# Turning the slots' token rows on VectorE, and packing expert weights from GpSimd, in a two-layer graph-attention and mixture-of-experts kernel

## The chip, the cores and the metric

The program runs on one core of one Trainium2 chip. The metric is the device time of one execution in microseconds (us), smaller is better. The engines of the core are named here as in the profile: PE is TensorE (matmuls; PEld is its weight load, which overlaps the matmuls), DVE is VectorE, ACT is ScalarE, POOL is GpSimd and SP is SyncE, which in this kernel does nothing but issue DMAs and read the registers they need. POOL and ACT can issue DMAs too.

## The reference

There are 2708 tokens of 256 numbers. Two layers follow one another; each has an attention over a graph (a 2708 by 2708 matrix of 0 and 1) and then a mixture of 8 experts of which every token uses two.

```python
# layer 0
x = x + elu(softmax(where(adj > 0, q @ k.T / 16, -9e15)) @ v)    # q, k, v from _layernorm(x)
# then, on t = _layernorm(x):
xn = layernorm(t)
xe[e] = xn * ln_g[e] + ln_b[e]
h = gelu(xe[e] @ W1[e] + b1[e])            # 256 -> 1024
y = h @ W2[e] + b2[e]                      # 1024 -> 256
x = x + sum over the top two experts of weight * y
# layer 1
x = x + softmax(where(adj > 0, s_src + s_dst, -1e9)) @ (t @ W_fc + b_fc)
x = x + sum over the top two experts of p_e * (gelu(t @ W1[e] + b1[e]) @ W2[e] + b2[e])   # 256 -> 512 -> 256
```

## The kernel before, in words

The work has five stages, one behind the other: attention of layer 0, expert slots of layer 0, attention of layer 1, expert slots of layer 1, and the final sum.

**Attention of layer 0** (`layer0_attention`). The queries are cut into six blocks of 512 (the last has 148); for each block `b` the loop runs over 22 key tiles `k`, and one pass of that loop is called a key step. A step computes the scores of one key tile on PE (L537), takes their exponential on ACT (L549), multiplies by the mask on DVE (L552), and adds the product with the values into accumulators on PE (L601), three steps later. Beside it, DVE makes the next block's masks out of integers loaded from `adj` (L386, L403, L409); the columns of the last two key tiles have their own small load, `load_apart` (L414), made in step 14 of a block and used by PE in steps 20 and 21 (L544, L576). One more job runs beside these steps, a list named `background` of which one entry is started every fifth step. Its entries are DMAs issued by SP: two fillers, and one `pack` for each of the 16 experts (8 in each layer), which copies that expert's `W1`, `W2`, `b2`, `b1` (and in layer 0 `ln_g`, `ln_b`) from their inputs into one DRAM row per partition, `packed`, by 4 or 6 DMAs (L1009 to L1025).

**Routing** (`route`, L1093). Each finished tile of 128 tokens is normalized (`norm_stats`, L245, which has one short POOL instruction, L256, and `normed`, L259), its two experts are chosen, and its rows are written by an indirect DMA from POOL (L1197) into `disp`, a DRAM tensor of 258 numbers per row: 256 of the token, then its index, then its weight. The rows of an expert are contiguous there. Routing is written as a generator whose pieces are placed between the steps of other work (`Line`).

**Slots** (`Experts.slots`, L1406). A slot is 128 rows of one expert. Layer 0 runs 45 of them, layer 1 runs 47, the last two of these inside a branch that is taken only when they are used. For a slot the kernel fetches weights (`fetch_weights`, L1356: an indirect DMA from POOL into one of 4 buffers, whose rows are skipped when the buffer already holds that expert) and rows (`fetch_rows`, L1373: one DMA of 128 rows of 1032 bytes from SP, into one of 6 buffers `xg`). Both are fetched three slots ahead (`AHEAD`). `turned` (L1410) turns the 128 by 256 rows into columns: two PE transposes against the identity into PSUM (L1414), then a copy out of PSUM, by DVE with the expert's own norm in layer 0 (L1418, two instructions) and by ACT in layer 1 (L1424). `up` multiplies by `W1` on PE (L1441) and takes the gelu on ACT (L1449); it also scales the bias, on DVE in layer 0 (L1432) and on ACT in layer 1 (L1434). `down` multiplies by `W2` on PE (L1457), and DVE scales and adds the bias (L1463); the result `y` goes out by an indirect DMA from POOL (L1469, L1476) at the row numbers that lie in `xg`. The PE work of `down` for one slot is put behind `up` of the next, so that ACT has time for the gelu.

The order of the instructions on each engine comes from a scheduler in layer 0, and from the order of the program on PE, ACT and DVE in the slots of layer 1 (L1399). SP's order is always that of the program.

Of the kernel before, what the change touches and what calls it, by code (L numbers as in the profile page):

```python
# [9 lines left out]
F32 = mybir.dt.float32  # L10
# [86 lines left out]
AHEAD = 3  # L97
DROW = D + 2
# [5 lines left out]
def adj_ffn_kernel(ctx: ExitStack, tc: tile.TileContext, a: dict, out: bass.AP):  # L104
# [156 lines left out]

    def to_columns(dst, src, r):

        tp = misc.tile([P, GROUP, P], F32, name="misc")
        for c in range(DC):
            nc.tensor.transpose(tp[:, c, :r], src[:, c * P : (c + 1) * P], ident[:r, :r])  # L266
        nc.scalar.copy(dst, tp[:, :DC, :r])
# [77 lines left out]
    def layer0_attention(line):  # L345
        with ExitStack() as scope, ExitStack() as until_last:
# [18 lines left out]
            xin = {}  # L365
# [164 lines left out]
            def scores(b, k, g, apart, mT):  # L530
                b0, nb, ts_ = BLOCKS[b]
                kr, k0 = ROWS[k], k * P
                if k == NT - 1:
                    return tail_scores(b, g, apart, mT)
                ps = ps_s.tile([P, BN], F32, name="s")
                for c in range(DC):
                    nc.tensor.matmul(  # L537
                        ps[:kr, :nb], xnT[:, c, k0 : k0 + kr], g[:, c, :nb],
                        start=(c == 0), stop=(c == DC - 1 and k < KEYS),
                    )  # L540
                if k >= KEYS:
                    for j, t in enumerate(ts_):
                        r = ROWS[t]
                        nc.tensor.matmul(  # L544
                            ps[:kr, j * P : j * P + r], apart[:, j, :kr], minus_big[:, :r],
                            start=False, stop=(j == len(ts_) - 1),
                        )
                p = of_block(b, "p", [P, nb], F32, bufs=6)
                nc.scalar.activation(p[:kr, :nb], ps[:kr, :nb], AF.Exp, scale=1.0 / 16.0)  # L549
                mask = MASKS[b].of_key(mT, k)  # L550
                if k < KEYS:
                    nc.vector.scalar_tensor_tensor(  # L552
                        p, p, LARGEST, mask, op0=ALU.min, op1=ALU.mult
                    )
                else:
                    nc.vector.tensor_scalar(
                        mask[:kr], ps[:kr, :nb], -BIG / 2, None, ALU.is_gt, saturate=False,
                    )
                return p

            def tail_scores(b, g, apart, mT):
# [23 lines left out]
                for n0, n1, r in parts_:  # L585
                    nc.scalar.activation(p[n0:n1, :r], ps[n0:n1, :r], AF.Exp, scale=1.0 / 16.0)
# [36 lines left out]
            def evict(b, accs, total):  # L623
                for j, t in enumerate(BLOCKS[b][2]):
                    raw = rows.tile([P, VALUES + 1], F32, name="raw", bufs=6)
                    (nc.scalar.copy if j % 2 else nc.vector.tensor_copy)(
                        raw[: ROWS[t], : D + 1], accs[j][: ROWS[t]]
                    )
                    line.add(finish(t, raw, total))
# [6 lines left out]
            for b, (b0, nb, ts_) in enumerate(BLOCKS):  # L636
# [4 lines left out]
                for k in range(NT):  # L641
# [10 lines left out]
                    if k == (0 if b == last else NT - 8):  # L652
# [21 lines left out]
                    if background and b > 0 and k % 5 == 1 and (b > 1 or k > 10):  # L674
                        background.pop(0)()
                    if b > 0:
# [322 lines left out]
    def pack_weights(name, hidden, own_norm):  # L999
# [9 lines left out]
        def pack(e):  # L1009
            to = packed[e * P : (e + 1) * P, :]  # L1010
            nc.sync.dma_start(
                to[:, :w2].rearrange("p (c h) -> p c h", c=DC),
                a[f"{name}_W1"][e].rearrange("(c p) h -> p c h", p=P),
            )
            nc.sync.dma_start(
                to[:, w2:b2].rearrange("p (f d) -> p f d", f=hc),
                a[f"{name}_W2"][e].rearrange("(f p) d -> p f d", p=P),
            )
            nc.sync.dma_start(to[:, b2:b1], a[f"{name}_b2"][e].partition_broadcast(P))
            nc.sync.dma_start(to[:, b1:ln], a[f"{name}_b1"][:, e, :])  # L1020
            if own_norm:
                with nc.allow_non_contiguous_dma(reason="a few small vectors"):
                    nc.sync.dma_start(to[:, ln : ln + DC], a[f"{name}_ln_g"][:, :, e])
                    nc.sync.dma_start(to[:, ln + DC : row], a[f"{name}_ln_b"][:, :, e])
        background.extend(partial(pack, e) for e in range(E))  # L1025
        return packed, hc, w2, b2, b1, ln, row

    class Experts:
        def __init__(self, layer, hidden, packed_weights, w_gate, gate_bias, own_norm, xd, disp, early):
# [7 lines left out]
            self.groups = [f"written{layer}", f"late{layer}", f"apart{layer}", f"after{layer}"]  # L1037
# [24 lines left out]
        def other_rows(self, start, late=True):  # L1062


            groups = [self.groups[0]] if late else []
            if self.begun:
                groups.append(self.groups[1])
            for group in groups:
                tc.declare_no_dep(start.ins, group=group, reason="other rows of disp")
                tc.add_to_no_dep_group(group, start.ins)  # L1070
# [22 lines left out]
        def route(self, t, x, logits=None):  # L1093
# [17 lines left out]
            if own_norm:  # L1111
                xt = rows.tile([P, D], F32, name="xn", bufs=4)[:r]
                normed(xt, x[:r], mean, once)
                normed(rows2[:r, 0, :D], x[:r], mean, twice)
            else:
                xt = rows2[:r, 0, :D]
                row = normed(xt, x[:r], mean, once)
# [201 lines left out]
        def begin_steps(self):  # L1319
# [3 lines left out]
            rows_ = [self.fetch_rows(s) for s in range(AHEAD)]  # L1323
            self.fetched = []
            for s in range(AHEAD):
                self.fetched.append((self.fetch_weights(s), rows_[s]))
# [46 lines left out]
        def fetch_rows(self, s):  # L1373
            disp = self.disp
            xg = self.one.tile([P, DROW], F32, name="xg", bufs=RING + 2)
# [5 lines left out]
            start = nc.sync.dma_start(xg, disp[bass.ds(at, P), :])  # L1381
            if s < FULL_AFTER[self.early]:
                self.other_rows(start, late=False)
            if s in (0, FULL_AFTER[self.early]):
                self.behind_written(start)
            return xg

        def run(self, line):
            with (
                self.scope,  # L1390
                tc.tile_pool(name="ffn2", bufs=2, side=self.side) as two,
                tc.tile_pool(name="ps_mm", bufs=2, space=PSUM) as ps_mm,
                tc.tile_pool(name="ps_tp", bufs=2, space=PSUM) as ps_tp,
                tc.tile_pool(name="ps_acc", bufs=2, space=PSUM) as ps_acc,
            ):
                with ExitStack() as order:
# [7 lines left out]
                    self.slots(two, ps_mm, ps_tp, ps_acc, line)  # L1404

        def slots(self, two, ps_mm, ps_tp, ps_acc, line):  # L1406
# [3 lines left out]
            def turned(s):  # L1410
                w, xg = self.fetched[s]
                tp = ps_tp.tile([P, GROUP, P], F32, name="tp")
                for c in range(DC):
                    nc.tensor.transpose(tp[:, c, :], xg[:, c * P : (c + 1) * P], ident)  # L1414
                xe = two.tile([P, DC, P], F32, name="xe")
                if own_norm:
                    for c in range(DC):
                        nc.vector.tensor_scalar(  # L1418
                            xe[:, c, :], tp[:, c, :],
# [3 lines left out]
                else:  # L1423
                    nc.scalar.copy(xe, tp[:, :DC, :])  # L1424
# [29 lines left out]
            def down(s, w, xg, hT, bias2, then):  # L1454
                ps = ps_acc.tile([P, D], F32, name="acc")
                for f in range(hc):
# [6 lines left out]
                nc.vector.scalar_tensor_tensor(  # L1463
                    y, ps, xg[:, D + 1 : D + 2], bias2, op0=ALU.mult, op1=ALU.add
                )
                at = bass.IndirectOffsetOnAxis(ap=xg.bitcast(I32)[:, D : D + 1], axis=0)
# [22 lines left out]
            def slot(s, s1):  # L1489
                nonlocal placed, behind, xe  # L1490
                w, xg = self.fetched[s]
# [4 lines left out]
                hT, bias2 = up(w, xe, xg[:, D + 1 : D + 2])  # L1496
# [4 lines left out]
                def fetch(behind_add=None):  # L1501
# [4 lines left out]
                    if s + AHEAD < SLOTS and s + AHEAD == len(self.fetched):  # L1506
                        self.fetched.append((
                            self.fetch_weights(s + AHEAD, behind_add), self.fetch_rows(s + AHEAD)
                        ))
# [16 lines left out]
                behind = (s, w, xg, hT, bias2)  # L1526
# [28 lines left out]
    background = []  # L1555
# [90 lines left out]
```

## Time and profile before

Six runs of the kernel have a median of 1245.55 us (1239.37 to 1250.77). The profiled execution took 1243.04 us, of which the profile shows a span of 1241.3 us.

| stage | from, us | to, us | PE busy, us |
|---|---|---|---|
| attention of layer 0 | 0 | 499 | 482.9 |
| slots of layer 0 | 499 | 837 | 335.0 |
| attention of layer 1 | 837 | 1014 | 171.5 |
| slots of layer 1 | 1014 | 1214.5 | 181.9 |
| final sum | 1214.5 | 1241.3 | 0 |

Over the span PE is busy for 1171.3 us, DVE for 539.7, ACT for 447.2 and POOL for 421.3. A line of a group of instructions reads: source line, engine, operation, output and inputs with their shapes, count, then busy time and the mean duration of one, then the idle time of the engine just ahead of them and what ended most of it. In a line of the timeline the first number is the start and the second the length of a run of like instructions, and a bracket gives the idle time ahead of it with what ended it. A busy PE is not PE at its peak, since matmuls are pipelined: what a matmul costs is the distance to the next start.

### The profile page before, as it was taken

The page shows a single profiled execution, that of the slowest core. Times are in us where ns is not written, and L with a number is a line of the kernel's source. Part 1 is how long each engine was busy: PE and PEld are TensorE (multiplying, and loading weights), DVE is VectorE, ACT ScalarE, POOL GpSimd, SP SyncE. Part 2 cuts the span into 40 slices and gives each one's busy share as a digit, 9 for nine tenths or more (in the row PEclk, how much of TensorE's full clock was granted, in tenths as well). Part 3 has the DMA queues.
Part 4 walks back from the last instruction along what each step waited for, and adds up shares of the span by engine and source line. Part 5 has one row for each costly group of instructions (what it writes and reads, how often), then busy time and mean ns, then how long its engine had stood idle before and what let it go on. Part 6 is the DMA issues. An engine that isn't in the chain of part 4 may idle for free. (4 is left out here: it accounts for less than half of the span.)

```text
span 1241.3 us, 20059 instructions
## 1 busy us (share of the span) xinstructions
PE 1171.3 (94%) x6712; PEld 941.2 (76%) x6712; DVE 539.7 (43%) x2055; ACT 447.2 (36%) x1301; POOL 421.3 (34%) x525
## 2 busy tenths in 40 slices
PE   8989999999999999999999999999999988899990
PEld 5656666666665675899999999987999977799880
DVE  5465762845456536631211121115867774211114
ACT  3222222222212222642233322324767657344440
POOL 3010020120211204343333333334635567455450
PEclk9999999999999999999999999998999999999995
DMA  9493973999997677475667745443004225644457
GB/s 201 67 182 83 166 171 113 200 215 228 217 192 168 131 174 261 138 210 141 226 203 230 271 124 176 111 107 92 2 10 156 102 65 192 173 142 139 136 183 276
DMA packets 148355, 197.83 MB, mean 159 GB/s; under 512 B 27595, under 2 KB 131748, under 8 KB 142104
## 3 DMA queue, kind: packets, MB, share of 16 engines
q1 hardware_dynamic: 120314, 110.16, 38.7%
q0 software_dynamic: 27040, 83.56, 21.8%
q10 hardware_dynamic: 894, 2.77, 0.6%
q8 instruction: 56, 0.92, 0.3%
q14 instruction: 51, 0.42, 0.1%
HBM read 263.66 MB, written 66.15 MB: 266 GB/s over the span
## 5 line engine op out<-in xcount | busy, mean ns | idle before, releaser
L1441 PE MATMUL mm<-xe,ring 128*128 128x128 f32 x2192 | 266.2, 278 | 15.4 <-ACT xe L1424 7.6
L1441 PEld LDWEIGHTS mm<-xe,ring 128*128 128x128 f32 x2192 | 255.2, 192 | 32.4 <-issue 19.2
L1457 PE MATMUL acc<-ring,hT 128*128 128x256 f32 x1096 | 261.3, 381 | 2.1 <-issue 1.6
L1449 ACT ACTIVATE hT<-mm,ring 128x128 f32<-128x128 f32 x548 | 156.0, 369 | 287.1 <-issue 179.7
L1463 DVE SCALAR_TENSOR_TENSOR y<-acc,xg,bias 128x256 f32<-128x256 f32 x92 | 44.5, 484 | 399.7 <-PE acc L1457 367.6
L1457 PEld LDWEIGHTS acc<-ring,hT 128*128 128x128 f32 x1096 | 198.4, 191 | 24.5 <-issue 1.9
L601 PEld LDWEIGHTS acc<-v,p 128*128 128x128 f32 (+1 forms) x880 | 159.5, 190 | 65.3 <-issue 41.0
L601 PE MATMUL acc<-v,p 128*128 128x257 f32 (+1 forms) x880 | 204.1, 384 | 2.4 <-DVE p L552 1.4
L537 PE MATMUL s<-g,xnT 128*128 128x512 f32 x420 | 202.6, 602 | 0.0
L1358 POOL DMA_INDIRECT ring<-L_ffn_packed,weight_row x98 | 103.5, 1056 | 185.2 <-issue 95.1
L256 POOL TENSOR_TENSOR ln_rs<-ln_rs,minus_half 128x2 f32<-128x2 f32 x88 | 66.0, 752 | 250.3 <-DVE ln_rs L252 212.2
L1197 POOL DMA_INDIRECT disp<-row,to x88 | 90.1, 1024 | 163.4 <-DVE to L1194 57.3
L844 PE MATMUL acc<-parts,m 128*128 128x266 f32 x924 | 127.6, 295 | 0.0
L549 ACT ACTIVATE p<-s 128x512 f32<-128x512 f32 x105 | 62.5, 595 | 180.5 <-PE s L537 145.4
L844 PEld LDWEIGHTS acc<-parts,m 128*128 128x128 f32 x924 | 118.2, 187 | 4.4 <-ACT raw L871 0.9
L537 PEld LDWEIGHTS s<-g,xnT 128*128 128x128 f32 x420 | 76.2, 192 | 53.7 <-issue 50.3
L552 DVE SCALAR_TENSOR_TENSOR p<-p,mT 128x512 f32<-128x512 f32 x100 | 68.4, 686 | 94.4 <-ACT p L549 91.0
L1476 POOL DMA_INDIRECT xd<-y,xg x45 | 71.4, 1586 | 87.1 <-issue 32.3
L811 ACT CAST m<-mT 128x512 fp32r<-128x512 fp8e4 (+4 forms) x168 | 71.9, 475 | 12.3 <-PE acc L844 7.2
L1469 POOL DMA_INDIRECT xd<-y,xg x47 | 47.0, 999 | 20.8 <-PE tp L1414 7.6
L403 DVE TENSOR_SCALAR m_rows<-adj 128x512 fp8e4<-128x512 int32 (+1 forms) x105 | 42.1, 433 | 2.0 <-DMA adj<-in_adj_dram 2.0
L1414 PE MATMUL tp<-ident,xg 128*128 128x128 f32 x184 | 35.1, 275 | 1.2 <-DMA xg<-disp 0.7
(252 smaller groups left out, 1080.1 us busy)
## 6 DMA issues: line engine op xcount, KB each, us to landing
adj<-in_adj_dram SPq DMA_DIRECT2D x100, 256.0 KB
L_ffn_packed<-in_L_ffn_W_dram SPq DMA_DIRECT2D x16, 1024.0 KB
xg<-disp SPq DMA_DIRECT2D x98, 129.0 KB
L_ffn_packed<-in_L_ffn_W_dram SPq DMA_DIRECT2D x16, 512.0 KB
neighbours<-mT SPq DMA_DIRECT2D x5, 1408.0 KB
mT<-neighbours SPq DMA_DIRECT2D x5, 1408.0 KB
xin<-in_x_dram SPq DMA_DIRECT2D x42, 128.0 KB
ring<-L_ffn_packed SPq DMA_DIRECT2D x4, 1154.0 KB
```

The costliest lines, as they stand in the source:

```text
L256: nc.gpsimd.tensor_tensor(rs[:r, 1], rs[:r, 0], minus_half[:r], ALU.pow)
L537: nc.tensor.matmul(ps[:kr, :nb], xnT[:, c, k0 : k0 + kr], g[:, c, :nb], start=(c == 0), stop=(c == DC - 1 and k < KEYS),)
L552: nc.vector.scalar_tensor_tensor(p, p, LARGEST, mask, op0=ALU.min, op1=ALU.mult)
L601: nc.tensor.matmul(accs[j][:r], p[keys, q0 : q0 + r], v[keys, k, :], start=(k == 0), stop=(k == NT - 1),)
L811: nc.scalar.copy(m[:, : q1 - q0], MASKS[b].of_key(mTs[b], k)[:, q0 - b * BN : q1 - b * BN],)
L844: nc.tensor.matmul(acc[:r], masks[t], parts[:, k, i], start=(k == 0 and i == 0), stop=False,)
L1197: nc.gpsimd.indirect_dma_start(disp[:], bass.IndirectOffsetOnAxis(ap=to[:r, j : j + 1], axis=0), rows2[:r, j], None,)
L1358: start = nc.gpsimd.indirect_dma_start(w, None, packed[:], bass.IndirectOffsetOnAxis(ap=self.weight_row[:, s : s + 1], axis=0), bounds_che ...
L1441: nc.tensor.matmul(ps[:, i, :], w[:, c * hidden + f * P : c * hidden + (f + 1) * P], xe[:, c, :], start=(c == 0), stop=(c == DC - 1),)
L1449: nc.scalar.activation(hT[:, f, :], ps[:, i, :], AF.Gelu, bias=w[:, b1 + f : b1 + f + 1])
L1457: nc.tensor.matmul(ps, hT[:, f, :], w[:, w2 + f * D : w2 + (f + 1) * D], start=(f == 0), stop=(f == hc - 1),)
L1476: start = nc.gpsimd.indirect_dma_start(xd[:], at, y, None, bounds_check=N - 1, oob_is_err=False, compute_op=ALU.add)
```

## The change

In the slots, PE no longer transposes the rows. DVE does it with its own transpose, which works on blocks of 32 by 32. For that, the token's numbers are written into `disp` in another order (`by_quarters`), and a slot's rows are loaded by four DMAs, each of which fills 32 partitions with pieces of 64 numbers (256 bytes), and a fifth that loads the last two numbers of each row into a buffer of its own, `who`. Rows are fetched five slots ahead, weights still three. In layer 0 the transpose of slots below 45 is put on DVE behind the result `y` of the slot two before (or, at the beginning, behind the copy of an accumulator of the attention). In layer 0 the norm now reads SBUF and not PSUM; in layer 1 the copy on ACT is gone. PSUM that held the transposes goes to `up`, which has 4 buffers and not 2.

The packing of the weights is cut into pieces (`W1`; `W2`; `b2` and `b1`; in layer 0 also `ln_g` and `ln_b`), 56 in all. From step 11 of block 1 on, each key step issues one piece, from POOL and not from SP, and each piece has to wait for the exponential of that step. `background` keeps the other entries. The small load `load_apart` is made in step 4 of a block and not in step 14.

```diff
+ROWS_AHEAD = 5
+    def in_chunks(x):
+        return x.rearrange("p (c g j) -> p g c j", c=DC, g=GROUP)
+    def by_quarters(row):
+        return row.rearrange("p (g c j) -> p g c j", g=GROUP, c=DC)
...
-                nc.scalar.activation(p[:kr, :nb], ps[:kr, :nb], AF.Exp, scale=1.0 / 16.0)
+                exp_of[0] = nc.scalar.activation(
+                    p[:kr, :nb], ps[:kr, :nb], AF.Exp, scale=1.0 / 16.0
+                )
...
+                    if j == 0:
+                        experts0.issued = copied
...
-                    if k == (0 if b == last else NT - 8):
+                    if k == (0 if b == last else GROUP):
                         apart = load_apart(b)
...
-                    if background and b > 0 and k % 5 == 1 and (b > 1 or k > 10):
+                    if background and b > 0 and k % 5 == 1:
                         background.pop(0)()
+                    if packing and b > 0 and (b > 1 or k > 10):
+                        for start in packing.pop(0)():
+                            tc.add_manual_dep(
+                                start.ins, exp_of[0].ins.name,
...
+                                reason="no sooner than this step",
+                            )
...
-            nc.sync.dma_start(
+        def pieces(e):
+            to, dma = packed[e * P : (e + 1) * P, :], nc.gpsimd.dma_start
+            yield lambda: [dma(
                 to[:, :w2].rearrange("p (c h) -> p c h", c=DC),
                 a[f"{name}_W1"][e].rearrange("(c p) h -> p c h", p=P),
-            )
+            )]
...
-        background.extend(partial(pack, e) for e in range(E))
+        for e in range(E):
+            packing.extend(pieces(e))
...
-                normed(rows2[:r, 0, :D], x[:r], mean, twice)
+                normed(by_quarters(rows2[:r, 0, :D]), in_chunks(x[:r]), mean, twice)
...
-            xg = self.one.tile([P, DROW], F32, name="xg", bufs=RING + 2)
+            disp, wide = self.disp, D // GROUP
+            xg = self.one.tile([P, GROUP, wide], F32, name="xg", bufs=ROWS_AHEAD + 2)
+            who = self.one.tile([P, 2], F32, name="who", bufs=ROWS_AHEAD + 3)
...
-            start = nc.sync.dma_start(xg, disp[bass.ds(at, P), :])
+            chunk = disp[bass.ds(at, P), :]
+            starts = [
+                nc.sync.dma_start(
+                    xg[g * QUARTER : (g + 1) * QUARTER],
+                    chunk[:, g * wide : (g + 1) * wide].rearrange("(t i) e -> i t e", t=GROUP),
+                )
+                for g in range(GROUP)
+            ]
+            starts.append(nc.sync.dma_start(who, chunk[:, D:]))
...
-                tc.tile_pool(name="ps_mm", bufs=2, space=PSUM) as ps_mm,
-                tc.tile_pool(name="ps_tp", bufs=2, space=PSUM) as ps_tp,
+                tc.tile_pool(name="ps_mm", bufs=4, space=PSUM) as ps_mm,
...
-                w, xg = self.fetched[s]
-                tp = ps_tp.tile([P, GROUP, P], F32, name="tp")
-                for c in range(DC):
-                    nc.tensor.transpose(tp[:, c, :], xg[:, c * P : (c + 1) * P], ident)
+                w, (xg, _) = self.weights[s], self.rows_[s]
                 xe = two.tile([P, DC, P], F32, name="xe")
+                raw = two.tile([P, DC, P], F32, name="xe_raw") if own_norm else xe
+                with tc.issue_after(self.issued.ins) if own_norm and s < OFTEN else ExitStack():
+                    nc.vector.transpose(
+                        raw.rearrange("p c (t i) -> p t c i", t=GROUP),
+                        xg.rearrange("p t (c j) -> p t c j", c=DC),
+                    )
                 if own_norm:
                     for c in range(DC):
                         nc.vector.tensor_scalar(
-                            xe[:, c, :], tp[:, c, :],
+                            xe[:, c, :], raw[:, c, :],
...
-                else:
-                    nc.scalar.copy(xe, tp[:, :DC, :])
...
-                nc.vector.scalar_tensor_tensor(
-                    y, ps, xg[:, D + 1 : D + 2], bias2, op0=ALU.mult, op1=ALU.add
+                self.issued = nc.vector.scalar_tensor_tensor(
+                    y, ps, who[:, 1:2], bias2, op0=ALU.mult, op1=ALU.add
                 )
...
+                    for _ in range(2):
+                        at = len(self.rows_)
+                        if at <= s + ROWS_AHEAD and at < (SLOTS if placed else n):
+                            self.rows_.append(self.fetch_rows(at))
```

## The prediction

> **What bounds the kernel now.** I read first the busy time of each engine in five stages, then, by waits, what PE waited for, then the timeline of one slot of each layer, and last the DMA queues and POOL where the change puts new work.
>
> Busy time by stage (columns: stretch, length, then busy time of PE, PEld, DVE, ACT, POOL, the granted clock, DMA share, GB/s):
>
> ```profile
> 120.00:360.00 240.00, 239.48 (x969) 157.55 (x964) 133.40 (x486) 54.81 (x123) 35.27 (x58) 1.00 0.91 186
> 360.00:400.00 40.00, 36.42 (x149) 22.00 (x148) 25.07 (x88) 8.82 (x20) 6.82 (x14) 0.96 0.91 197
> ...
> 499.00:837.00 338.00, 335.03 (x2284) 305.20 (x2284) 79.93 (x285) 116.90 (x383) 125.08 (x102) 1.00 0.59 176
> ...
> 1014.00:1062.00 48.00, 38.76 (x269) 34.46 (x269) 25.16 (x128) 34.36 (x83) 32.80 (x39) 1.00 0.48 151
> ...
> 1100.00:1200.00 100.00, 97.49 (x674) 91.11 (x674) 12.58 (x26) 47.40 (x156) 53.04 (x52) 1.00 0.45 144
> ```
>
> PE is the bound nearly everywhere, in the slots too (335.0 of 338 us, 97.5 of 100), while DVE there works a quarter or an eighth of the time. So an instruction taken off PE in a slot is worth its full pitch, if nothing comes late in its place. Only 1014 to 1062 has real holes (9.2 us).
>
> One slot of layer 0 (PE and DVE):
>
> ```profile
> 564.27 2.76 PE L1457 MATMUL acc<-ring,hT 128*128 128x256 f32 x12
> ...
> 566.86 0.38 PE L1414 MATMUL tp<-ident,xg 128*128 128x128 f32 x2
> ...
> 567.06 0.48 DVE L1463 SCALAR_TENSOR_TENSOR y<-acc,xg,bias 128x256 f32<-128x256 f32 x1 [5.96 <-PE acc L1457]
> 567.08 1.03 PE L1457 MATMUL acc<-ring,hT 128*128 128x256 f32 x4
> ...
> 567.46 0.72 DVE L1418 TENSOR_SCALAR xe<-tp,ring 128x128 f32<-128x128 f32 x2
> ...
> 567.97 3.81 PE L1441 MATMUL mm<-xe,ring 128*128 128x128 f32 x32
> ```
>
> Starts, not lengths, carry the cost: the two transposes hold PE from 566.86 to 567.08, 0.22 us; an acc matmul has a pitch of (566.86 - 564.27) / 12 = 0.216 us. The slot repeats every 7.35 us. In layer 1 the same two cost 0.22 us of a pitch of 3.73.
>
> The one hole late in the first attention, and the waits of PE in the slots of layer 1:
>
> ```profile
> 374.38 0.40 PE L544 MATMUL s<-minus_big,apart 128*128 128x128 bf16 x4 [3.02 <-DVE apart L424]
> ```
> ```profile
> PE mm L1441 <- ACT xe L1424: 7.6, 8, 2.4
> PE mm L1441 <- DMA ring<-L_ffn_packed,weight_row: 4.8, 4, 2.5
> ...
> PE tp L1414 <- DMA xg<-disp: 0.7, 1, 0.7
> ```
>
> **The change, part by part.**
>
> *Layer 0 slots.* Removed: 45 x 0.22 = 9.9 us of PE. New: a chain on DVE behind y. In the built order DVE runs y, transpose, bias, two norms; PE runs four matmuls of `down` (8 passes, 8 x 0.216 = 1.73 us) between the end of the older slot's sums and the next `up`. From the timeline: y starts 0.20 after that end, the next DVE instruction 0.40 later, so the transpose starts at 0.60; successive DVE instructions overlap by 0.08. The transpose of 256 columns isn't in this trace. Nearest rows: the mask transposes, 0.396 us for 128 columns, 0.345 for 160 columns in another layout, and 1.06 ns per further element (DVE's 1024-column add 1.224 us less its 256-column one 0.407, over 768). I take 0.345 + 96 x 1.06 ns = 0.45, because 32 neighbours lie together as there; the upper end is twice 0.396 = 0.79. Then the bias (0.345) starts at 0.97, the first norm at 1.24 and ends at 1.52 (0.28: L260's 0.413 less 128 x 1.06 ns), before 1.73; the second ends at 1.72, needed at 1.95. No stall. At the upper end (0.79, norms 0.36 as now) the second ends at 2.22: 0.27 us late in 43 slots, +11.6. The first slot's rows now wait for the accumulator's copy and the transpose on the same engine: +0.5 (0 to 1). Sum taken -9.4, between -9.9 and +2.7.
>
> *Layer 1 slots.* Removed: 47 x 0.22 = 10.3 us. DVE puts the transpose ahead of the older y and has most of its time free, so nothing is late in the steady part. ACT loses 47 copies of 0.387 us; eight of PE's waits, 7.6 us, are for that copy, which stands behind gelu and table loads of the last routings. PE can now go on to `up`, but `down` still needs the gelu from the same busy ACT: I take -4 (-7.6 to 0). The wait for xg, 0.7, goes: xg is free after the transpose, not after the scatter. What is late next is the weights: their fetch is issued at a slot's `down` and has until three slots later; each slot is 0.22 shorter, so the four waits grow by about 2 x 0.22 each, +1.8, and more traffic delays them; I take +3 (0 to +14, below). Sum taken -12.0.
>
> *Row loads.* One DMA of 128 pieces becomes five with 640. DMA time per piece: in 1100 to 1200 the hardware queue's 3553 packets took 12.5% of 16 engines, 56 ns for 918 bytes; the software queue's 4804 took 32.2%, 107 ns for 2288. The line through both gives 32 ns for 256 bytes and 22 for 8: 512 x 32 + 128 x 22 over 16 engines = 1.19 us per slot against 0.48 now. Layer 1's share goes from 0.45 to about 0.45 + 0.71 / 3.51 = 0.65: hidden by the prefetch, except where weights arrive in bursts. The upper end: 45 ns per piece makes 1.8 us, 38% of a pitch, in the four bursts +3.5 each, the +14 above. SP issues five DMAs, not one: 0.333 each now, 0.321 for the adj loads of the same shape (L390), plus 0.07 of register work and 0.27 for the token read: 5 x 0.40 + 0.27 = 2.3 us, under 3.51. On SP it moves past nothing but fillers and five mask loads.
>
> The Trainium skill, "DMA: Bandwidth & Descriptors", section "Specifications", says that a piece needs 512 bytes for line rate, and that the engine does a read-modify-write below that; this speaks against pieces of 256. If a piece then costs what 512 bytes cost in the adj stretch (about 41 ns: 22 to 32 us, share 0.97, 196 GB/s), the sum would move only inside the +3 to +14.
>
> *The transpose on DVE.* The Trainium skill, "VectorE: DVE Perf Modes", section "The three transpose paths" and its rules, advises TensorE for a full 128 by 128 turn where PSUM will do; by it the gain of both layers would be nil. It weighs one turn alone; the trace here has PE at 97% and DVE at 13 to 24%, so I go by the rows.
>
> *The small load, step 4.* PE's 3.02 us wait for apart goes, and some of the lower clock behind it (0.83 in 370 to 380, where PE was busy 6.4 us: 1.1). Taken -3.5 (-4.1 to 0). In block 0 it stands on DVE before mask work at about 72 us with its load issued some 10 us sooner: 0.
>
> *Packing on POOL.* SP loses 80 DMAs (16 x (0.59 + 0.62 + 0.97 + 0.60) + 8 x 1.25 = 54 us), which stood between mask loads; PE loses almost nothing to masks today, so 0. POOL gains the 80, each waiting for an exponential. Behind the waiting piece stand the norm's power (L256), the index copies and the scatters; DVE waits in order for that power, and the masks of p stand behind it; PE feels it after three steps, about 11.7 us. Price: unknown here. The only plain POOL DMA takes 0.75 us for 128 short rows. If that is a fixed price, an expert of layer 0 (6 DMAs) takes 4.5 us; if by rows (2048), 12. Block 2 issues 21 such pieces, 5.25 experts: 24 to 63 us beside the 12.5 that POOL was busy in 205 to 285, in 86 us. Both fit, so I take 0, with -1 to +10. The bytes and nearly their time (158 to 375 us against 171 to 446) stay.
>
> Sum: -9.4 - 10.3 - 4 - 0.7 + 3 - 3.5 + 0 = -24.9. On the profiled execution's 1243.04 that is 1218.1; the median of the runs shown is 2.5 us higher, so 1221.
>
> **The rivals.**
>
> *DVE chain late.* The transpose costs 0.79, not 0.45: layer 0 gains nothing, 1221 + 11.6 = 1233. For it: the 128-column row's slow layout; against: the 160-column row.
>
> *Weights behind small pieces.* +11 in layer 1: 1232. For it: DMA is at nine tenths or more in the bursts around 1135 to 1155; against: three slots of prefetch.
>
> *POOL late in packing.* It decides from (86 - 12.5) / 5.25 = 14 us per expert on; 20 us make POOL 31 late in block 2, of which 12 are hidden: 1221 + 19 = 1240. Against: both ends of the price lie below 14.
>
> *The other side: SP bounds the slots of layer 1.* Five issues per slot, register work included, need (3.51 - 0.27) / 5 = 0.65 us or less each. Beyond, 47 slots are paced by SP; at 0.78 the loss is 47 x 0.65 = 30 us, and from there on the kernel is slower. At 1.0 us: 5.27 per slot, +83, 1304. For it: L386 has a median of 0.626 (four times the pieces, with the queue full) and single ones of 4.7; against: 0.333 and 0.321 for 128 pieces.
>
> *It doesn't do what it says.* Not here: the built order has no transpose on PE in the slots.
>
> **How the numbers follow.** Main 0.58, DVE chain 0.14, weights 0.10, POOL 0.10, SP 0.08. Half a per cent, 6.2 us, is about what runs of this kernel can tell from no change. Faster (below 1239.3): 0.57 + 0.12 + 0.08 + 0.02 = 0.79. Same: 0.01 + 0.02 + 0.02 + 0.04 = 0.09. Slower (above 1251.8): 0.04 of POOL and 0.08 of SP, 0.12. The main case has 1210 to 1230; the range reaches to 1243 to take in the DVE chain, the weights and half of POOL, and leaves out 0.18: 1209 to 1243.
>
> **What would show it.** No L1414-like matmul on PE; slots of layer 0 every 7.13 us and of layer 1 every 3.51; the DVE transpose at 0.45; no wait for apart; fewer waits for ACT in 1014 to 1062. I am wrong if PE waits for DVE's xe each slot, if SP's issues touch one another through layer 1, or if POOL's DMAs in 160 to 380 fill it and PE waits for p.

## The result, and the profile after

The changed kernel took 1249.92 us (median of 21 runs, 1246.03 to 1258.36), the kernel before 1244.82 (47 runs): a ratio of 1.0049, 95% interval 1.0036 to 1.0061. I had said 1221. The profiled execution of after has a span of 1254.2 us, 12.9 more than before; it lies 6.1 above the median of its kernel and that of before 1.8 below, so the profiles show a larger loss than the 5.1 us between the medians.

The gain in the slots is there; it was spent ahead of them. This table cuts both spans at the same places, each taken at its start: the last matmul of the full blocks of the first attention, which are the five of 512 queries (L601, after L613), the first matmul of a slot (L1441, L1484), and the results `y` (L1463, L1506).

| stretch, us | before | after | difference |
|---|---|---|---|
| start to the end of the last full block | 460.5 | 481.2 | +20.7 |
| from there to the first slot's matmul | 39.5 | 50.3 | +10.8 |
| to the last `y` of layer 0 | 335.0 | 330.3 | -4.7 |
| to the first `y` of layer 1 | 185.3 | 180.6 | -4.7 |
| to the last `y` of layer 1 | 193.1 | 184.0 | -9.1 |
| to the end | 28.0 | 27.9 | -0.1 |

The slots first. One slot of layer 0 in after's timeline:

```profile
644.51 3.62 PE L1500 MATMUL acc<-ring,hT 128*128 128x256 f32 x16
...
646.45 0.48 DVE L1506 SCALAR_TENSOR_TENSOR y<-acc,who,bias 128x256 f32<-128x256 f32 x1 [5.44 <-PE acc L1500]
646.85 0.43 DVE L1457 STREAM_TRANSPOSE xe_raw<-xg 128x256 f32<-128x256 f32 x1
647.20 0.32 DVE L1475 TENSOR_SCALAR bias<-ring,who 128x256 f32<-128x256 f32 x1
647.43 0.60 DVE L1463 TENSOR_SCALAR xe<-xe_raw,ring 128x128 f32<-128x128 f32 x2
...
647.97 3.73 PE L1484 MATMUL mm<-xe,ring 128*128 128x128 f32 x32
```

The 16 `acc` matmuls run through, and the next `mm` follows at their pitch: PE waits for nothing. The transpose takes 0.43 us. The median distance from `y` to `y` fell from 7.35 to 7.03 us in layer 0 and from 3.73 to 3.51 in layer 1.

Now the loss. Waits of after between 120 and 530 us (in all, times, the longest), and the busy time by stretch with the columns of the prediction:

```profile
DVE m_rows L411 <- DMA adj<-in_adj_dram: 26.1, 2, 13.6
...
DVE bias L1475 <- DMA who<-disp: 13.2, 1, 13.2
...
PE misc L1177 <- ACT gT L275: 13.0, 1, 13.0
...
PE acc L613 <- DVE p_last L562: 9.0, 1, 9.0
...
PE acc L613 <- DVE p L562: 6.0, 1, 6.0
```
```profile
240.00:300.00 60.00, 53.52 (x208) 34.27 (x207) 26.18 (x97) 9.89 (x23) 26.02 (x35) 0.94 1.04 228
300.00:360.00 60.00, 46.99 (x169) 30.22 (x168) 31.45 (x118) 11.47 (x26) 18.65 (x31) 0.86 1.06 223
```

Two holes. The first is new: twice DVE waits 12 to 14 us for the rows of `adj` from which it makes masks, and PE, three steps later, runs dry: 19.5 us idle in 240 to 360, and a granted clock of 0.86 in the second stretch. PE's longest wait, 13.0 us up to 335.4, is for ACT's copy `gT` of the routing; ACT had itself stood 17.0 us, up to 334.7, for DVE. Before, PE lost 0.5 us in these stretches, and DVE did not wait for `adj` at all after the first 100 us:

```profile
240.00:300.00 60.00, 59.48 (x244) 38.31 (x242) 26.86 (x97) 12.71 (x29) 8.81 (x11) 1.00 1.05 207
300.00:360.00 60.00, 60.00 (x226) 40.18 (x225) 35.26 (x126) 13.48 (x30) 10.17 (x16) 1.00 1.02 211
```

The DMA share is about 1 in both kernels. SP's timeline of after shows the loads that are late, at the starts of the second and the third full block after the first, and below them the latter place in before:

```profile
231.41 20.80 SPq L394 DMA_DIRECT2D adj<-in_adj_dram  x4
...
298.06 32.12 SPq L394 DMA_DIRECT2D adj<-in_adj_dram  x8
```
```profile
308.01 14.51 SPq L386 DMA_DIRECT2D adj<-in_adj_dram  x8
```

Eight issues in 32 us, against 14.5 us before: SP stands in the issues themselves, of which single ones take up to 9.3 us. I take it that its queue doesn't drain; no view shows the queue's length.

The second hole lies at 509 to 518 us, just ahead of the slots. Timelines of SP, DVE and PE in after:

```profile
494.99 3.32 SPq L1416 DMA_DIRECT2D xg<-disp  x4
498.50 0.35 SPq L1422 DMA_DIRECT2D who<-disp  x1
499.39 1.86 SPq L1416 DMA_DIRECT2D xg<-disp  x4
506.64 0.35 SPq L1422 DMA_DIRECT2D who<-disp  x1
...
517.58 0.35 DVE L1475 TENSOR_SCALAR bias<-ring,who 128x256 f32<-128x256 f32 x1 [13.17 <-DMA who<-disp]
...
518.53 2.20 PE L613 MATMUL acc<-v,p_last 128*128 128x257 f32 x4 [8.98 <-DVE p_last L562]
```

The scheduler has put the bias of slot 0 on DVE ahead of the last masks of the attention. The bias reads `who`, and `who` lands at 517.5, 19 us after it was issued. Behind the bias stand the masks, behind the masks PE. From 498 to 513 us the queues moved (packets, MB, share of 16 engines):

```profile
q0 software_dynamic: 381, 6.09, 97.9%
q1 hardware_dynamic: 320, 0.07, 2.3%
```

q0 carries the weights of the first slots, 381 packets of 16 KB in the mean (349 are rows of 17 KB), and q1 the pieces of the token rows, 640 for each slot. While the weights streamed, 320 packets of q1 went through in 15 us. The first of them moved at 500.5, and from there to 513 us the counts of the two queues are 324 and 320: the packets of the two pass one for one. In e5, the same kernel run again, they are 310 and 310 from 480 to 492 us. In the 5 us after 513, with most weights landed, 1264 went through.

### The profile page after: what moved, and what is told of

Same layout as the page of the kernel before. It is cut to its first block, busy times and chain, and to the rows that moved or that the text cites. A ratio compares the mean times of both kernels' runs of the same rounds, so it can differ in the third digit from the quotient of the medians.

```text
span 1254.2 us, 21045 instructions
## 1 busy us (share of the span) xinstructions
PE 1158.3 (92%) x6528; PEld 933.8 (74%) x6528; DVE 564.6 (45%) x2147; ACT 434.1 (35%) x1254; POOL 480.1 (38%) x605
## 5 line engine op out<-in xcount | busy, mean ns | idle before, releaser
L1484 PE MATMUL mm<-xe,ring 128*128 128x128 f32 x2192 | 268.9, 280 | 15.9 <-DMA ring<-L_ffn_packed,weight_row 6.8
L1484 PEld LDWEIGHTS mm<-xe,ring 128*128 128x128 f32 x2192 | 262.2, 195 | 28.1 <-issue 14.2
L1500 PE MATMUL acc<-ring,hT 128*128 128x256 f32 x1096 | 256.5, 383 | 4.3 <-ACT hT L1492 3.1
L1500 PEld LDWEIGHTS acc<-ring,hT 128*128 128x128 f32 x1096 | 202.6, 192 | 29.7 <-ACT hT L1492 4.1
L613 PEld LDWEIGHTS acc<-v,p 128*128 128x128 f32 (+1 forms) x880 | 161.4, 192 | 71.5 <-issue 41.6
L613 PE MATMUL acc<-v,p 128*128 128x257 f32 (+1 forms) x880 | 206.8, 387 | 7.5 <-DVE p L562 7.5
L1506 DVE SCALAR_TENSOR_TENSOR y<-acc,who,bias 128x256 f32<-128x256 f32 x92 | 44.5, 483 | 352.1 <-PE acc L1500 344.0
L1519 POOL DMA_INDIRECT xd<-y,who x45 | 71.4, 1588 | 115.6 <-issue 61.1
L1512 POOL DMA_INDIRECT xd<-y,who x47 | 47.2, 1003 | 21.5 <-issue 12.9
L613 PE MATMUL acc<-v,p_last 128*128 128x257 f32 (+3 forms) x88 | 27.1, 409 | 9.0 <-DVE p_last L562 9.0
```

The source lines that it names most:

```text
L613: nc.tensor.matmul(accs[j][:r], p[keys, q0 : q0 + r], v[keys, k, :], start=(k == 0), stop=(k == NT - 1),)
L1484: nc.tensor.matmul(ps[:, i, :], w[:, c * hidden + f * P : c * hidden + (f + 1) * P], xe[:, c, :], start=(c == 0), stop=(c == DC - 1),)
L1500: nc.tensor.matmul(ps, hT[:, f, :], w[:, w2 + f * D : w2 + (f + 1) * D], start=(f == 0), stop=(f == hc - 1),)
L1519: start = nc.gpsimd.indirect_dma_start(xd[:], at, y, None, bounds_check=N - 1, oob_is_err=False, compute_op=ALU.add)
```

## The experiments

**First theory.** The packing makes the mask rows late. The rival is that another part does (the small load at step 4, the row loads). Four kernels on one chip.

e1 gives the packing back to SP, whole experts at every fifth step:

```diff
-                    if packing and b > 0 and (b > 1 or k > 10):
-                        for start in packing.pop(0)():
...
+                    if background and b > 0 and k % 5 == 1 and (b > 1 or k > 10):
+                        background.pop(0)()
```

> After, with the packing as it was before (whole experts, one per five steps, on SP's queue between the mask loads); all else stays. Theory 1 (the new packing makes mask rows late in the first attention): the two waits of DVE for adj of 13 us each go, the attention's last full block ends near 461 instead of 481, and the kernel is about 20 us faster than after, near 1230. Rival (the mask rows are late because of the small load at step 4 or because of the new row loads): it stays at 1250 +- 4.

Measured: 1.0001 of before (0.9973 to 1.0029). DVE has no wait for `adj`, and the full blocks end at 452.6. But the built order differs in hundreds of places on PE and DVE: 28 fewer matmuls lie ahead of that end, so its time can't be set beside the others; the first weights are fetched at 501.6 (474 before), and the first slot starts 20.8 us after the attention. The half on masks is as expected; as a measure of the packing's price it fails.

e2 puts the new packing alone into the kernel before:

```diff
...
-        background.extend(partial(pack, e) for e in range(E))
+        for e in range(E):
+            packing.extend(pieces(e))
```

> Before, with the new packing alone (pieces on POOL, one per key step, each bound to that step's exponential); slots, small load and row loads as before. Theory 1: about 20 us slower than before, near 1265, with waits of DVE for adj of 10 us and more after 240 us. Rival (packing is harmless, something else in after is the cause): 1245 +- 4.

Measured: 1.0014 (0.9995 to 1.0033). DVE waits four times for `adj`, 18.7 us in all, but PE loses only some 5 us in 240 to 360, and the full blocks end at 459.7. So the new packing alone brings the waits, but on this chip not their price: my 20 us were wrong for it.

e3 keeps the packing on POOL at the old pace:

```diff
-                    if packing and b > 0 and (b > 1 or k > 10):
-                        for start in packing.pop(0)():
+                    if packing and b > 0 and k % 5 == 1 and (b > 1 or k > 20):
+                        for start in [s_ for piece in packing.pop(0) for s_ in piece()]:
...
```

> After, with the packing still on POOL and bound to an exponential, but a whole expert at every fifth step, as the old one was paced. If the pace is the cause (56 steps for 16 experts instead of 80, when the DMA engines are full), most of the 20 us come back: 1230 to 1234. If the queue is the cause (POOL's software queue shares the DMA engines with the mask rows instead of standing in line with them), it stays slow, 1245 to 1252, with the same long waits for adj. If POOL's own lateness is the cause, also slow, but with waits for ln_rs and not for adj.

Measured: 1.0119 (1.0089 to 1.0149), full blocks at 488.0, four waits of DVE for `adj`, 22.6 us in all. PE's holes moved with the bursts (stretches of e3):

```profile
220.00:240.00 20.00, 11.18 (x40) 6.93 (x38) 6.46 (x21) 2.03 (x4) 3.09 (x7) 0.87 1.08 191
240.00:260.00 20.00, 16.72 (x56) 10.84 (x57) 16.75 (x70) 4.76 (x13) 9.18 (x15) 0.78 1.15 223
...
320.00:340.00 20.00, 9.00 (x31) 5.64 (x30) 6.99 (x25) 1.77 (x4) 4.84 (x11) 0.76 1.13 211
```

So a slower mean pace does not help if an expert's 4 or 6 DMAs come at once on POOL's queue where a block's mask loads begin. It speaks for the shared DMA engines and against POOL's time.

e4 loads `who` ahead of the four blocks:

```diff
-            starts = [
+            starts = [nc.sync.dma_start(who, chunk[:, D:])]
+            starts += [
...
-            starts.append(nc.sync.dma_start(who, chunk[:, D:]))
```

> After, with the 8-byte who rows of a slot loaded ahead of its four blocks of rows instead of behind them. Theory: the 13.2 us wait of DVE's bias for who near 505 to 517, behind which the last masks of the attention stand, came from who standing last in SP's queue; it shrinks to a few us and the kernel is about 9 us faster than after, near 1241. Rival (the first slots' weights fill the DMA engines and hold back anything issued then): the wait stays over 8 us and the kernel at 1250 +- 3.

Measured: 0.9896 (0.9867 to 0.9925). The bias of slot 0 is free now (at 483.6 us), but that of slot 1 waits 11.9 us in its place, so the order inside a slot does not remove the wait; the first slot starts 45.4 us after the full blocks, against 50.0 to 51.3 in four executions of after. And the full blocks end at 460.5, although every instruction up to there has the order that it has in after. That was the surprise of this round: the 20.7 us were not a property of the program alone.

**Second round.** Is after itself always slow? And if small pieces are served slowly while weights stream, what does it bring to hold the weights back?

> The changed kernel once more, unaltered, beside the next three on one chip. Its instruction order through the first attention is the same as that of the kernel with who first, which ended that attention's full blocks at 460.5 us where after ended them at 481.2. If the 20.7 us belong to the packing on POOL (an unsteady race between two queues, met or missed by one execution), this run may show either value and its times spread over 10 us or more: between 1225 and 1250. If they belong to after as built, the full blocks end at 481 +- 3 again and the ratio is 1.005 again.

Measured: after, unaltered, on another chip than in the first round: 0.989 (0.9869 to 0.9912), 1224.53 us. Full blocks at 460.2, one wait for `adj` of 10.2 us; the wait for `who` (13.5) is there.

e6 makes the first three weight fetches of each layer wait for the rows of its first three slots; e7 does that and loads `who` first.

```diff
...
-                self.weights.append(self.fetch_weights(s))
+                self.weights.append(self.fetch_weights(s, first))
...
```

> After, with the weights of the first three slots of each layer fetched only when the rows (blocks and who) of those three slots have landed. Theory 2 (small pieces of rows are served slowly while weight rows stream from POOL's queue: 1550 pieces in 20 us, 0.2 us per piece and engine instead of the 0.03 of my estimate): the rows land within 5 us, the 13 us wait of the bias for who is below 3 us, and the first slot starts within 3 us of the attention's end: 10 to 14 us faster than after. Rival (who is late because its own chain, the scatters it reads behind, is late): no change of the wait, and the weights' delay adds 5 us.

> Both: who ahead of the blocks, and the first weights behind the first rows. Theory 2: the order inside a slot's rows hardly matters once the weights stay away, so within 3 us of the kernel with the weights behind the rows alone. If who first is what counts: as fast as that kernel was, 0.99 of before, with or without the weights held.

Measured: 0.9878 (0.9854 to 0.9903) and 0.9859 (0.9833 to 0.9885). No wait for `who` is left in either, and the bias no longer stops the masks. What DVE waits for in e6 between 480 and 515 is the weights:

```profile
DVE xe L1468 <- DMA ring<-L_ffn_packed,weight_row: 3.6, 1, 3.6
```

The mechanism is confirmed, and nearly the price: from the full blocks' end to the first slot e6 and e7 take 41.9 and 42.0 us, e5 51.3, so 9 us of the 10 to 14 came. Yet the kernels gain only 0.2 and 2.4 us on e5, within their intervals, for the edit holds the first weights back in layer 1 too. There PE now waits for them ahead of the first slot, 7.5 us in e6 and 6.6 in e7, where e5 has no such wait:

```profile
PE mm L1489 <- DMA ring<-L_ffn_packed,weight_row: 7.5, 1, 7.5
```

From the last `y` of layer 0 to the first of layer 1 e6 and e7 take 188.7 and 188.9 us, e5 179.6. Why the slots of layer 1 take another 5 us in e7 (182.7 against 177.6) stays open.

e6 shows something else. Up to the full blocks' end it has the order of e5 on every engine, and it ran on the same chip, yet its full blocks end at 465.6 (460.2 in e5) and DVE waits three times for `adj`, 15.5 us in all (once, 10.2). The mask rows come in time or late from one execution to the next.

e8 adds the old packing to e7.

> The same two edits, and the packing as before on SP. If the packing on POOL costs the attention about 20 us in after, this is the fastest of the four, near 1215 where before is 1240; if the packing costs little (before with the new packing alone was 1.0014), it is within 4 us of the kernel with the two edits alone.

Measured: 1.0105 (1.0075 to 1.0135). As in e1 no wait for `adj`, full blocks at 452.4 with fewer matmuls ahead of them; and as in e1 the built order brings the first slot late, 27.9 us after the attention. A miss that tells nothing of the packing's price.

**Third round: how much slack is there?** e9 is after again, e12 the kernel before, both on one chip. e10 gives after 14% more packing, and otherwise the same order on every engine:

```diff
...
+                dma(
+                    spare[e * P : (e + 1) * P, :512].rearrange("p (c h) -> p c h", c=DC),
+                    a[f"{name}_W1"][e, :, :256].rearrange("(c p) h -> p c h", p=P),
+                ),
```

> The changed kernel, unaltered, a third time. Two results stand against each other: 1.0049 of before on record, with two waits of DVE for mask rows (12.5 and 13.6 us) and full blocks done at 481.2 us; 0.989 in the repeat, with one such wait (10.2) and 460.2. In the stretch 240 to 360 the recorded execution moved 228 and 223 GB/s with the DMA engines full, the repeat 241 and 237. Theory: the packing on POOL leaves the mask rows no slack there, so some per cent of DMA speed decide; then here too one wait and about 0.989 where the stretch moves near 240 GB/s, two waits and about 1.005 where it moves near 225.

> The kernel before, unaltered, for its trace on this chip. If the chip of the recorded executions had the slower DMA, before too moves more here in the full stretch than the 207 and 211 GB/s that it had in 240 to 300 and 300 to 360, and is some us faster than 1243; if the speed of the DMA is the same, 207 and 211 again, and the recorded result of after has another cause.

> After, with one more copy of 256 KB per expert (a quarter of W1 in layer 0, half in layer 1) into a spare tensor, in the step that copies the biases; every engine's order is otherwise the same. It adds about 0.25 of 1.77 MB per expert, 14% of the packing and some 7% of all DMA work between 165 and 360 us. Theory (no slack): a second long wait of DVE for mask rows appears at the start of the third full block, the full blocks end 15 to 25 us later than in the repeat of after, near 480, and the kernel is 15 to 25 us slower than the repeat. Rival (the DMA engines have room, the recorded time came from something else): less than 4 us slower.

Measured: e9 0.993 (0.9905 to 0.9955), one wait of 9.4 us, full blocks at 459.9. e10 1.0036 (1.0016 to 1.0055), 13.1 us slower than e9 (the forecast began at 15), three waits of 20.9 us in all, full blocks at 475.3. The stretches of e9, of e12, and of e10:

```profile
240.00:300.00 60.00, 56.46 (x222) 36.51 (x221) 26.84 (x98) 10.62 (x25) 26.64 (x33) 0.97 1.02 247
300.00:360.00 60.00, 60.00 (x230) 38.91 (x229) 40.57 (x155) 15.35 (x36) 28.24 (x42) 1.00 0.97 236
```
```profile
240.00:300.00 60.00, 59.48 (x243) 38.33 (x242) 27.16 (x98) 12.78 (x28) 8.66 (x11) 1.00 1.05 240
```
```profile
300.00:360.00 60.00, 48.62 (x178) 31.46 (x177) 34.48 (x131) 11.76 (x28) 24.32 (x39) 0.89 1.05 252
```

With full engines, before moves 240 GB/s here in 240 to 300 us and moved 207 in the profiled execution of the result, one program and one order. Over 165 to 430 us the two queues of after in that first execution, of e9 and of e10 show:

```profile
q0 software_dynamic: 9555, 30.38, 48.4%
q1 hardware_dynamic: 30371, 20.56, 37.4%
```
```profile
q0 software_dynamic: 9747, 30.91, 44.0%
q1 hardware_dynamic: 30686, 20.92, 34.7%
```
```profile
q0 software_dynamic: 10863, 34.63, 49.4%
q1 hardware_dynamic: 30546, 20.80, 35.4%
```

In the first execution of after 1.7% fewer MB cost 85.8% of the engines' time, in e9 78.7%: a MB was 11% dearer. With 7% more MB, e10 stands at 84.8% and falls into the same hole at the start of the third block. The eight loads at that block's start take SP 32.1 us in the first execution and 15.2 in e9. So where the DMA is quicker the packing leaves the mask rows just enough, and there is no slack: 7% more work brings back most of the 20.7 us. That slower DMA made the second wait in the result is inferred from this: no experiment ran at that speed.

e11 is e7 with a piece at two of three steps:

```diff
-                    if packing and b > 0 and (b > 1 or k > 10):
+                    if packing and k % 3 != 0 and b > 0 and (b > 1 or k > 10):
```

> The kernel with who first and the weights behind the first rows (0.9859 of before), with a piece of packing at two of three key steps instead of each. Theory: a third less packing per us leaves the mask rows slack; the 10.5 us wait for adj shrinks below 5, the 7 us of holes that PE has in 240 to 300 go, and the kernel is 3 to 8 us faster, 0.980 to 0.984. Rival (the waits come from bursts at a block's start, whatever the mean pace): no change, 0.986, or slower because the packing now ends beside the last block.

Measured: 0.9824 (0.9788 to 0.986), 1216.34 us, no wait for `adj`, full blocks at 454.5, first slot at 498.5. It beats before, and e9 by 11.9 us.

**Fourth round: the pace alone.** e13 makes the edit just shown on after and no other; e14 adds e10's copy to it; e16 is after. e15 takes back the step of the small load:

```diff
-                    if k == (0 if b == last else GROUP):
+                    if k == (0 if b == last else NT - 8):
```

> After, with a piece of packing at two of three key steps, and nothing else changed. If the pace alone makes the mask rows late: no wait of DVE for adj over 2 us, full blocks done near 454 instead of 460, 5 to 8 us faster than after beside it; the 13 us wait of the bias for who stays. If the two other edits did it: same as after within 3 us.

> The same, with the extra 256 KB copy per expert that cost after 13 us. If the slower pace gives slack: within 4 us of the kernel without the copy, waits for adj below 4 us in all. If slack is still lacking: 10 us and more slower, with a wait at the start of the third full block.

> After, with the small load of a block's own key rows back at step NT - 8. My prediction priced the move at -3.5 us: so 2 to 5 us slower than after, PE waiting 3 us for apart once near 375. Rival (the move puts the load among the mask loads and delays them): equal or faster than after, with shorter waits for adj.

> After, unaltered, as the measure for the three kernels beside it: 0.989 to 0.993 of before with one wait for adj of some 10 us where the DMA engines move about 240 GB/s in 240 to 300 us; 1.005 and two such waits where they move about 225.

Measured beside e16 (0.9916, 0.9886 to 0.9946; 1227.88 us): e13 0.9883 (0.9852 to 0.9914), e14 0.9872 (0.9842 to 0.9901). In e13 and e14 DVE has no wait for `adj`, and the full blocks end at 454.3 and 453.3 (459.7 in e16). The stretches of e13:

```profile
240.00:300.00 60.00, 60.00 (x246) 38.79 (x245) 27.38 (x103) 12.63 (x29) 21.26 (x26) 1.00 0.76 197
300.00:360.00 60.00, 60.00 (x229) 39.91 (x228) 40.40 (x155) 14.67 (x34) 25.21 (x37) 1.00 0.91 204
```

PE is busy all through, with DMA at 0.76 and 0.91. And the extra copy that cost after 13 us costs nothing at the slower pace. So with the packing on POOL's queue its pace decides whether the mask rows come late, here where DMA is quick; at the speed of the result it was not tried. PE's order up to there is that of after; DVE's differs in some fifty places. The 5 us at the full blocks' end are 4.5 in the median, a little under the forecast, and the intervals of e13 and e16 overlap: the trace shows the gain more surely than the time does. The wait for `who` (17.6 us in all) stays, as expected.

e15, with the small load back at step 14, takes 0.9898 (0.986 to 0.9936): not slower than after. Full blocks at 457.7, three waits for `adj` of 11.6 us in all (one of 8.7 in e16). PE has no wait for `apart` in it.

## Why the prediction was wrong

**Packing on POOL, taken at 0 (-1 to +10): the step that failed.** I wrote that SP loses 80 DMAs and PE almost nothing to masks, "so 0", and then priced POOL's time alone. POOL was never the matter: its DMAs take 0.54 to 0.91 us by their medians, 4.15 per expert of layer 0, under the low end of my 4.5 to 12. What I left out is that the 80 DMAs used to stand in one queue with the mask rows, one expert in five steps, and now come from a second queue, an expert in three and a half, into a stretch where the DMA share was already 0.91 and more. I had that number in the first fence, and put down "the bytes and nearly their time stay" as if that closed the matter; my own figures beside it, 217 us against 275, are 27% more packing per us (211 us in e9, 30%). In the profiled execution of the result the stretch grew by 20.7 us, and by more than that through late rows, since the wait for `apart` is gone from it: e13, with neither wait, ends it at 454.3. In e5, e9 and e16, on three chips, the full blocks of after ended at 459.7 to 460.2, as they do in before (460.2 in e12), but with a wait of 9 to 10 us already there and nothing left over. The Trainium skill, "DMA: Bandwidth & Descriptors", section "Queues, rings and completion order", says that each DMA engine takes turns between the queues that have work, a packet at a time. The trace agrees where pieces and weight rows meet, one for one (320 and 324 packets from 500.5 to 513 us). That the packing took its turns from the mask rows in the same way is argued from this: it had 60% of the engines' time in 240 to 330 us, however urgent the mask rows were. What makes it more than an argument is that more packing brings a long wait back (e10) and slower packing removes the waits (e13, e14). My rival of a late POOL named the right victim and the wrong cause, with a threshold (14 us per expert) that had nothing to do with it.

**The first slot's rows, +0.5: the second failure.** It was +10.8, and +11.1 between e12 and e9. I asked what stands behind the transpose and not what stands behind the bias, which reads `who` on the same engine. And I priced a piece of 256 bytes by its own time, 32 ns (45 at most). Its own time is 17 ns (2.3% of 16 engines x 15 us / 320), under every price that I had, but while the weights streamed an engine passed one per 750 ns (16 x 15 us / 320), since a packet of weights of 617 ns in the mean (97.9% x 16 x 15 us / 381) went between. A slot has 40 pieces per engine; 20 of them took these 15 us. e6 shows that this is the cause: with the weights held back the wait for `who` is gone. My rival had weights late behind pieces; it was the pieces behind the weights.

**Layer 0 slots, -9.4: right in kind, short in size.** Each steady slot gained 0.32 us, not 0.22 (44 x 0.32 = 14.1); beside the transposes 0.08 went with the break in PE's stream, from `mm` start to `acc` start (3.65, now 3.57). DVE's chain caused no stall, the transpose took 0.43 for my 0.45. The first slots, whose rows are late, gave part back: -10.9 between e12 and e9, -4.7 in the result. The advice of TensorE for full turns (the Trainium skill, "VectorE: DVE Perf Modes", section "Rules for kernel authors"), which I set aside by the rows, would have missed this gain.

**Layer 1 slots, -12.0: right.** The pitch is the 3.51 of my forecast. From the last `y` of layer 0 to the last of layer 1 the result shows -13.8, and e9 against e12 -10.7. The wait for ACT's `xe` is gone; waits for weights grew from 4.8 to 6.8 us, for my +3. Three waits for DVE's `xe`, 3.4 us in all, are new and stood in no sum of mine. In after, from 1014 us on:

```profile
PE mm L1484 <- DMA ring<-L_ffn_packed,weight_row: 6.8, 3, 3.5
...
PE mm L1484 <- DVE xe L1457: 3.4, 3, 1.3
```

**The small load, -3.5: the gain came, but the move was not needed for it.** The wait of 3.0 us for `apart` is gone, and e13, without late rows, ends the full blocks 5.9 us sooner than e12. But undone, the move costs nothing (e15): with the packing off SP's queue the load is in time at either step, in e2 as well. Whether the move alone would do, with the packing still on SP, no clean run shows; e1, which has it so, has no such wait, but another order. **SP** never paced the slots: from 1100 to 1200 us its 144 issues took 43.5 us.

Summed over one chip (the profiled e9 less e12): -0.3 +11.1 -10.9 -1.6 -9.1 +0.3 = -10.5 us; the medians there differ by 8.7. With the first slot's rows at +0.5 it would have been -21, near my -24.9. So where the DMA is quick the second step alone takes nearly half of the gain that I forecast; in the result the first takes the rest and more.

## What to carry to other kernels

Before moving background DMAs to another queue or a faster pace, look at the DMA share of the stretch that they go to, and name the loads there that have a due time; the moved ones will take turns with them. Price a small piece by the turn that it waits for when a big transfer runs beside it, not by its bytes. And where a margin is that thin, one set of executions need not agree with another: measure how much extra load it takes to bring the stall.

## What the runs showed of the hardware

DMA speed differed between executions of one program, before: 207 GB/s in the result and 240 in e12, in 240 to 300 us with full engines. In the next 60 us the order is turned (211 at a share of 1.02, 173 at 0.87), for e12 was done sooner; over 165 to 430 us 49.18 MB cost 89.3% of the engines' time in the one and 49.48 MB 84.1% in the other, 7% more per MB. The time of before differs by only 0.6% (1244.82 and 1236.94). Whether the chip or the moment makes the difference, no run shows. After, with no slack, went from 0.989 to 1.005 of before. The Trainium skill, "HBM Reference", section "Specifications (TRN2)", says that two cores share the bandwidth of a domain; no run here shows whether a neighbour was busy.

While a queue with rows of 17 KB and one with pieces of 256 bytes both had work, their packets passed one for one, so a piece of 17 ns advanced once in some 0.6 us (16 x 12.5 us / 320, after, 500.5 to 513 us).
